# Expert blocks of two halves in turns, and each weight fetch issued between a block's products and its bias add

## The chip, the cores and the metric

One core of one Trainium2 chip runs the whole program. The metric is the device time of one execution in microseconds (us). The engines named below are PE (TensorE, matrix products), DVE (VectorE), ACT (ScalarE), POOL (GpSimd, which here mainly issues transfers) and SP (SyncE, transfers only). Each engine works through its own queue in order. A difference of about 0.3% is what a measurement of this kernel can tell from none.

## The reference, cut to what matters

Eight items of 256 channels by 32x32 positions go through a multi-head attention layer with a residual, then through a single-head attention layer, then through a mixture of experts. The last part is the one that the change touches:

```python
logits = tokens @ router_w.T                 # 8 experts
probs = softmax(logits); rw, re = top_k(probs, 2); rw = rw / rw.sum(-1)
combine = zeros((N, E)).at[arange(N)[:, None], re].set(rw)
out = tokens
for e in range(8):
    h = gelu(tokens @ w1[e] + b1[e], approximate=False)   # 256 -> 256
    y = h @ w2[e] + b2[e]                                 # 256 -> 256
    out = out + combine[:, e:e + 1] * y
```

A token is one position of one item, 1024 tokens an item. Each token needs only the two experts that its router chose. The setup makes `b1` and `b2` all zeros.

## The kernel before, in words

Items 0 to 7 are worked on one after the other: `layer0` (the multi-head attention), `attend` (the single-head one), `normed` and the router. For items 0 to 6 `dispatch` (L847) scatters each token's normalised row twice, once for each chosen expert, into a DRAM buffer `rows` that has one region for each expert. The eighth item isn't dispatched: its experts are computed densely at the end (`dense`), every expert for every token.

In the middle of item 7's `layer0` the function `plan` (L924) cuts the filled part of each region into blocks of 256 rows, on DVE, from the counts. Their number is only known on the chip, so the program has a fixed number of positions, `group.nb` = 63, and `plan` fills two tables: `row_at`, the first row of the block at each position, and `w_at`, the rows of the packed weights `wpack` to fetch for it. Blocks stand in the order of their experts: all blocks of expert 0, then all of expert 1, and so on.

`experts` (L1018) then runs the positions b = 0 to 62. Per position:

- `fetch` (L1036): SP reads the block's start and loads its 256 rows in four transfers into `xr` (four buffers).
- `weights` (L1025): POOL issues one indirect transfer of 128 rows of 5128 bytes (both matrices and both biases of one expert, 656,384 bytes) into buffer b mod 4 of `wbs_x` (`wb` three times, `wb_x`). If the block four positions earlier belonged to the same expert, the buffer already holds the right weights; `plan` then sets the indices out of bounds (L979, L982), and the transfer is issued but moves no rows. Below this is called a skipped fetch, the other a real one.
- `turned` (L1047): DVE turns `xr` into `xb` (two buffers).
- `hidden` (L1056): PE makes 8 products into `ph` (L1061), ACT applies the Gelu (L1071).
- `collect` (L1080): PE makes 8 products into `pe` (L1087, two buffers in PSUM), DVE adds the bias `b2` out of the same `wb` buffer and writes `yb` (L1097, two buffers), POOL issues the store of `yb` into the DRAM buffer `y` (L1102). Then one step of `places` may run.

The loop at the end of `experts` sets the order by hand, and `tc.issue_after` pins some instructions:

```python
for b in range(group.nb + 4):
    if b - 3 in rows: hiddens[b - 3], last = hidden(b - 3, rows.pop(b - 3))
    if b < group.nb:  rows[b] = fetch(b)
    if b - 1 in rows: weights(b - 1)
    if b - 2 in rows: rows[b - 2], squares = turned(b - 2, rows.pop(b - 2))
    if b - 4 in hiddens: collect(b - 4, hiddens.pop(b - 4), last, squares)
```

So PE does the hidden products of position k+1, then the second products of k, then the hidden ones of k+2, and so on. On POOL the fetch for position k+4 stands behind the store of position k. The framework adds the waits from the order in which the code reads and writes each buffer: a fetch into a buffer waits for its earlier readers, and a reader waits for the last fetch that the code wrote above it.

`places` (L991) works out, on DVE, in which row of `y` each token's two results lie. It is a generator that gives way after each of its 14 pieces (7 items, 2 choices), 5 small instructions each; one piece runs in the iterations from position 4 on. Later, in item 7's last part, `Results` gathers these rows from `y` by POOL's indirect transfers (L1181) and adds them to the tokens.

Of the kernel before, what the change touches and what calls it, by code (L numbers as in the profile page):

```python
# [10 lines left out]
F32 = mybir.dt.float32  # L11
I32 = mybir.dt.int32
AF = mybir.ActivationFunctionType
ALU = mybir.AluOpType
# [5 lines left out]
def kernel(  # L20
# [23 lines left out]
    nc = tc.nc  # L44
    P = 128
    B, C, S = x.shape
    E, D, FF = w1.shape
# [4 lines left out]
    NT = S // P  # L52
# [5 lines left out]
    BR = R * P  # L58
    WROW = NCC * FF + NFC * D + NFC + D
    NWB = 3  # L60
    NXB = NWB + 1
    SQ = 32
    NQ = P // SQ
    DQ = D // NQ
    RUN = BR // SQ

    dram = ctx.enter_context(tc.tile_pool(name="dram", bufs=1, space=bass.MemoryType.DRAM))
    const = ctx.enter_context(tc.tile_pool(name="const", bufs=1))
# [4 lines left out]
    small = ctx.enter_context(tc.tile_pool(name="small", bufs=6))  # L73
    rowp = ctx.enter_context(tc.tile_pool(name="rowp", bufs=4))
    keep = ctx.enter_context(tc.tile_pool(name="keep", bufs=8))
# [64 lines left out]
    for e in range(E):  # L140
# [6 lines left out]
    NBMAX = max(2 * len(g) * S // BR + E - 1 for g in GROUPS)  # L147
    b_iota = const.tile([P, NBMAX], F32, name="b_iota")
    nc.gpsimd.iota(
        b_iota, [[1, NBMAX]], base=0, channel_multiplier=0, allow_small_or_imprecise_dtypes=True  # L150
    )
    p_iota = const.tile([P, 1], F32, name="p_iota")
    nc.gpsimd.iota(
# [10 lines left out]
        base=0,  # L164
        channel_multiplier=-1,
# [758 lines left out]
    def plan(group):  # L924


        n, nb, cap = group.n, group.nb, group.cap
        counts = group.counts
        steps = cap // BR

        def tmp(tag, shape, dtype=F32):
            return small.tile([P, *shape], dtype, tag=tag, name=f"{tag}_{n}", bufs=1)


        below = tmp("p_below", [E, steps])
        edge = tmp("p_edge", [steps])
        nc.vector.tensor_scalar_mul(edge, b_iota[:, :steps], float(BR))
        nc.vector.tensor_tensor(
            below,
            counts.unsqueeze(2).to_broadcast([P, E, steps]),  # L940
            edge.unsqueeze(1).to_broadcast([P, E, steps]),
            ALU.is_gt,
        )
        blocks = tmp("p_blocks", [E])
        nc.vector.tensor_reduce(blocks, below, AX.X, ALU.add)
        ends = tmp("p_ends", [E])
        nc.vector.tensor_tensor_scan(ends, ones[:, :E], blocks, 0.0, ALU.mult, ALU.add)
        first = keep.tile([P, E], F32, tag="first", name=f"first_{n}", bufs=2)
        nc.vector.tensor_sub(first, ends, blocks)

        mine = tmp("p_mine", [nb, E])
        of = b_iota[:, :nb].unsqueeze(2).to_broadcast([P, nb, E])
        nc.vector.tensor_tensor(
            mine, of, ends.unsqueeze(1).to_broadcast([P, nb, E]), ALU.is_ge
        )
        e_of = tmp("p_e", [nb])
        nc.vector.tensor_reduce(e_of, mine, AX.X, ALU.add)
        nc.vector.tensor_scalar_min(e_of, e_of, float(E - 1))
        nc.vector.tensor_tensor(
            mine,  # L960
            e_of.unsqueeze(2).to_broadcast([P, nb, E]),
            e_iota.unsqueeze(1).to_broadcast([P, nb, E]),
            ALU.is_equal,
        )

        base = tmp("p_base", [E])
        nc.vector.tensor_scalar_mul(base, first, -float(BR))
        work = tmp("p_work", [nb, E])
        lo, hi = tmp("p_lo", [nb]), tmp("p_hi", [nb])
        nc.vector.tensor_mul(work, mine, base.unsqueeze(1).to_broadcast([P, nb, E]))  # L970
        nc.vector.tensor_reduce(lo, work, AX.X, ALU.add)
        nc.vector.scalar_tensor_tensor(lo, b_iota[:, :nb], float(BR), lo, ALU.mult, ALU.add)
        nc.vector.tensor_scalar_min(lo, lo, float(cap - BR))
        nc.vector.scalar_tensor_tensor(lo, e_of, float(cap), lo, ALU.mult, ALU.add)
        row_at = keep.tile([P, NBMAX], I32, tag="row_at", name=f"row_at_{n}", bufs=2)
        nc.vector.tensor_copy(row_at[:, :nb], lo)
        nc.vector.tensor_scalar(hi, e_of, float(P), p_iota, ALU.mult, ALU.add)
        same = tmp("p_same", [nb])
        nc.vector.tensor_tensor(  # L979
            same[:, NXB:], e_of[:, NXB:], e_of[:, : nb - NXB], ALU.is_equal  # L980
        )
        nc.vector.scalar_tensor_tensor(  # L982
            hi[:, NXB:], same[:, NXB:], float(E * P), hi[:, NXB:], ALU.mult, ALU.add
        )
        w_at = keep.tile([P, NBMAX], I32, tag="w_at", name=f"w_at_{n}", bufs=2)
        nc.vector.tensor_copy(w_at[:, :nb], hi)

        group.first = first
        group.where = row_at, w_at

    def places(group):  # L991

        first = group.first
        for b in group.items:
            gate, kept = group.kept[b]
            ats = []
            for k, (row, exp) in enumerate(kept):
                hot = small.tile([P, NT, E], F32, tag="d_sel", name=f"p_hot_{b}_{k}", bufs=1)
                nc.vector.tensor_tensor(
                    hot,  # L1000
                    exp.unsqueeze(2).to_broadcast([P, NT, E]),
                    e_iota.unsqueeze(1).to_broadcast([P, NT, E]),
                    ALU.is_equal,
                )
                nc.vector.tensor_mul(
                    hot, hot, first.unsqueeze(1).to_broadcast([P, NT, E])
                )
                to = small.tile([P, NT], F32, tag="d_to", name=f"p_to_{b}_{k}", bufs=2)
                nc.vector.tensor_reduce(to, hot, AX.X, ALU.add)
                nc.vector.scalar_tensor_tensor(to, to, float(BR), row, ALU.mult, ALU.add)  # L1010
                at = keep.tile([P, NT], I32, tag=f"yat{k}", name=f"yat{k}_{b}")
                nc.vector.tensor_copy(at, to)
                ats.append(at)
                if k > 0:
                    group.kept[b] = gate, ats
                yield

    def experts(group, behind):  # L1018
        n = group.n
# [5 lines left out]
        def weights(b):  # L1025
            wb = wbs_x[b % NXB]
            nc.gpsimd.indirect_dma_start(
                out=wb[:, :],
                out_offset=None,
                in_=wpack[:, :],  # L1030
                in_offset=bass.IndirectOffsetOnAxis(ap=w_at[:, b : b + 1], axis=0),
                bounds_check=E * P - 1,
                oob_is_err=False,
            )
# [45 lines left out]
        def collect(b, hT, last, squares):  # L1080
            wb = wbs_x[b % NXB]
            py = acc(f"pe_{n}_{b}")
            at = NCC * FF
            with tc.issue_after(last.ins):
                for r in range(R):
                    for fc in range(NFC):
                        nc.tensor.matmul(  # L1087
                            py[:, ts(r, D)],
                            hT[:, fc, ts(r, P)],
                            wb[:, at + fc * D : at + (fc + 1) * D],  # L1090
                            start=(fc == 0),
                            stop=(fc == NFC - 1),
                        )
            at += NFC * D + NFC
            yb = two.tile([P, R, D], F32, tag="yb", name=f"yb_{n}_{b}")
            with tc.issue_after(squares.ins):
                added = nc.vector.tensor_add(  # L1097
                    yb,
                    py.rearrange("p (r d) -> p r d", d=D),
                    wb[:, at : at + D].unsqueeze(1).to_broadcast([P, R, D]),  # L1100
                )
            nc.gpsimd.dma_start(group.y[ts(b, BR), :].rearrange("(r p) d -> p r d", r=R), yb)  # L1102
            if b >= NXB:
                with tc.issue_after(added.ins):
                    next(placed, None)


        rows, hiddens = {}, {}
        placed = places(group)
        assert group.nb - NXB >= 2 * len(group.items)  # L1110
        last = squares = None
        for b in range(group.nb + 4):
            if b - 3 in rows:
                hiddens[b - 3], last = hidden(b - 3, rows.pop(b - 3))
            if b < group.nb:
                rows[b] = fetch(b)
            if b - 1 in rows:
                weights(b - 1)
            if b - 2 in rows:
                rows[b - 2], squares = turned(b - 2, rows.pop(b - 2))  # L1120
            if b - 4 in hiddens:
                collect(b - 4, hiddens.pop(b - 4), last, squares)
# [247 lines left out]
    for b in range(B):  # L1370
# [6 lines left out]
        if b + 1 < B:  # L1377
            begun = Begin(b + 1, next_x)
            t2 = attend(b, t1, begun.at)
            n2, _, l = normed(b, t2, begun.at)  # L1380
# [61 lines left out]
```

## Time and profile before

| what | us |
|---|---|
| time of the kernel, median of 3 runs (2348.14 to 2354.57) | 2354.15 |
| the profiled execution's own time | 2357.7 |
| its span, first to last instruction | 2355.1 |
| the expert stage: from the second products of position 0 to those of position 62 | 1885.8 to 2129.8 |
| PE busy in that stage of 244.0 | 222.4 |
| DVE / ACT / POOL busy in that stage | 97.4 / 54.8 / 108.5 |

The granted TensorE clock was 0.990 over the span. A row of the profile names the line, the engine, the operation and the tiles (written<-read); "idle before" is the time the engine waited ahead of it, and the name behind the arrow is what ended that wait. The chain of waits is followed back from the last instruction and printed in order of time: start, length, what. A transfer that POOL issues shows on POOL only as the time of its issue; its data and its completion come later.

### The profile page before, as it was taken

What the parts mean: (1) busy time and instruction counts of PE and PEld (TensorE: products, weight loads), DVE (VectorE), ACT (ScalarE), POOL (GpSimd) and SP (SyncE); (2) the same over time, 40 slices, a digit from 0 to 9 for tenths busy, and PEclk for the clock granted to TensorE, in tenths of its full rate; (3) what the DMA queues carried; (4) which work ended last, traced back from release to release, by engine and by line L of the source; (5) the groups of instructions that cost most, each with busy time, mean ns of one, the idle gap of its engine ahead of it and who ended that gap; (6) DMA issues with size and microseconds to landing.
All of it is one profiled execution on the core that took longest, in us unless ns stands there. A gap on an engine that the chain in (4) does not pass through costs nothing.

```text
span 2355.1 us, 37660 instructions
## 1 busy us (share of the span) xinstructions
PE 2282.4 (97%) x13123; PEld 1230.8 (52%) x13123; DVE 1512.9 (64%) x3660; ACT 1093.5 (46%) x1955; POOL 409.9 (17%) x390
## 2 busy tenths in 40 slices
PE   9999999999999999999999999999999998989698
PEld 3345534653456345633563356335643477776465
DVE  5775578557855785578557865786578653335755
ACT  3663366346634663466346635563555521223311
POOL 0000012000200020002000300030003044445563
PEclk9999999999999999999999999999999999999799
DMA  8995201020102010201020102000201268765564
GB/s 294 385 386 143 64 17 40 12 52 13 44 8 56 10 46 5 59 8 48 1 51 15 53 1 45 19 35 3 45 19 59 55 196 221 210 198 160 158 206 116
DMA packets 278756, 209.25 MB, mean 89 GB/s; under 512 B 187784, under 2 KB 230440, under 8 KB 276776
## 3 DMA queue, kind: packets, MB, share of 16 engines
q1 hardware_dynamic: 252472, 139.14, 21.0%
q0 software_dynamic: 25008, 67.20, 8.8%
q8 instruction: 104, 1.70, 0.3%
q10 hardware_dynamic: 1088, 0.52, 0.1%
q14 instruction: 84, 0.69, 0.1%
HBM read 108.88 MB, written 110.90 MB: 93 GB/s over the span
## 4 chain that ended last, share of the span: by engine, by line
PE 87%; DVE 4%; DMA 3%; issue 3%; ACT 1%; POOL 1%; SPq 0%; another core or an unknown queue 0%; DVEq 0%; POOLq 0%; ACTq 0%
PE po L539 19%; PE psc L462 18%; PE ps L670 9%; PE py L711 8%; PE pqk L344 7%; PE pr L636 5%; PE pv L381 4%; PE ph L1061 4%; PE pe L1087 3%; PE pdh L1308 2%; PE pdy L1332 2%; PE px L655 2%; DMA wb<-wpack,w_at 2%; PE pqk L322 2%; DVE n L236 1%
## 5 line engine op out<-in xcount | busy, mean ns | idle before, releaser
L503 ACT ACTIVATE ex<-psc,nmax 128x1024 f32<-128x1024 f32 x512 | 570.5, 1115 | 307.2 <-DVE scrap L486 220.9
L462 PE MATMUL psc<-qk,qk 64*64 64x512 f32 x4096 | 574.1, 593 | 3.4 <-ACT ex L503 3.3
L539 PE MATMUL po<-ex,vs 64*64 64x512 f32 x4096 | 569.6, 593 | 7.5 <-SPq L549 6.6
L486 DVE TENSOR_SCALAR_CACHE_REDUCE scrap<-psc,nmax 128x512 f32<-128x512 f32 x512 | 384.5, 751 | 163.9 <-PE psc L462 137.3
L477 DVE TENSOR_REDUCE nmax<-psc 128x1 f32<-128x512 f32 x512 | 350.7, 685 | 9.5 <-PE psc L462 9.5
L462 PEld LDWEIGHTS psc<-qk,qk 64*64 64x64 f32 x4096 | 178.8, 132 | 281.1 <-ACT ex L503 131.8
L539 PEld LDWEIGHTS po<-ex,vs 64*64 64x64 f32 x4096 | 173.4, 132 | 283.9 <-issue 84.2
L711 PE MATMUL py<-n,aT 128*128 128x256 f32 x1024 | 234.3, 383 | 4.5 <-DMA aT<-sq 4.5
L670 PE MATMUL ps<-nT,xa 128*128 128x512 f32 x512 | 228.5, 592 | 0.0
L711 PEld LDWEIGHTS py<-n,aT 128*128 128x128 f32 x1024 | 196.4, 193 | 54.9 <-issue 27.6
L915 POOL DMA_INDIRECT rows<-n,d_at x112 | 109.2, 975 | 661.4 <-DVE nmax L477 661.1
L695 ACT COPY aT<-sq 32x256 f32<-32x256 f32 x384 | 154.4, 402 | 79.8 <-DVE sq L688 52.3
L842 POOL TENSOR_TENSOR t<-t,n 128x2048 f32<-128x2048 f32 x8 | 36.3, 4535 | 879.2 <-DVE n L236 879.2
L344 PE MATMUL pqk<-xT,wqkv 128*128 128x512 f32 x384 | 171.2, 599 | 0.0
L670 PEld LDWEIGHTS ps<-nT,xa 128*128 128x128 f32 x512 | 96.6, 190 | 102.4 <-issue 95.1
L678 DVE TENSOR_REDUCE nmax<-ps 128x1 f32<-128x1024 f32 x64 | 77.9, 1217 | 88.3 <-PE ps L670 82.6
L309 ACT ACTIVATE qk<-pqk,b_qks 128x512 f32<-128x512 f32 x124 | 85.6, 690 | 95.8 <-PE pqk L344 77.0
L381 PE MATMUL pv<-wqkv,xT 128*128 128x512 f32 x256 | 121.5, 603 | 2.6 <-ACT wqkv L110 1.7
L1181 POOL DMA_INDIRECT yk<-y,yat x112 | 110.7, 988 | 74.6 <-issue 32.3
L344 PEld LDWEIGHTS pqk<-xT,wqkv 128*128 128x128 f32 x384 | 71.0, 190 | 99.9 <-issue 76.8
L1061 PE MATMUL ph<-xb,wb 128*128 128x256 f32 x384 | 95.3, 392 | 18.5 <-DMA wb<-wpack,w_at 15.6
L636 PE MATMUL pr<-wo,res 128*128 128x256 f32 x512 | 111.9, 379 | 0.0
(188 smaller groups left out, 2320.7 us busy)
## 6 DMA issues: line engine op xcount, KB each, us to landing
rows<-wb SPq DMA_DIRECT2D x7, 8192.0 KB
xr<-rows SPq DMA_DIRECT2D x252, 64.0 KB
y<-yb POOLq DMA_DIRECT2D x63, 256.0 KB
aT<-sq SPq DMA_DIRECT2D x384, 32.0 KB
xs<-in_x_dram SPq DMA_DIRECT2D x64, 128.0 KB
out_dram<-oT SPq DMA_DIRECT2D x60, 128.0 KB
xT<-in_x_dram SPq DMA_DIRECT2D x7, 1024.0 KB
sums<-t SPq DMA_DIRECT2D x7, 1024.0 KB
```

The costliest lines, as they stand in the source:

```text
L344: mm = nc.tensor.matmul(pq[:, ts(n, 512)], wqkv[:, cc, t, ts(g, P)], xT[:, cc, ts(n, 512)], start=(cc == 0), stop=(cc == NCC - 1),)
L381: nc.tensor.matmul(pv, self.xT[:, cc, ts(i, P)], wqkv[:, cc, 2, :], start=(cc == 0), stop=(cc == NCC - 1),)
L462: mm = nc.tensor.matmul(pss[at, h][ts(c, DK), ts(n, 512)], k[r, j * P + c * DK : j * P + (c + 1) * DK], q[r, ts(n, 512)], start=True, stop ...
L477: firsts[at, h] = nc.vector.tensor_reduce(nmax, pss[at, h][:, ts(0, 512)], AX.X, ALU.max, negate=True)
L486: seconds[h] = nc.vector.tensor_scalar(scrap, pss[at, h][:, ts(1, 512)], -1.0, nmaxes[at, h], ALU.mult, ALU.min, accum_out=nmax,)
L503: nc.scalar.activation(ex, pss.pop((at, h)), AF.Exp, bias=nmaxes.pop((at, h)), scale=1.0, accum_out=sums[at][:, h : h + 1],)
L539: mm = nc.tensor.matmul(po[n][ts(h, DK), :], vss[at][keys, h, :], exps[at, h][keys, ts(n, 512)], start=(j == 0 and turn == 0), stop=(j == ...
L636: nc.tensor.matmul(pr[:, :C], res[:, g, ts(i, P)], wo[:, g, :], start=(g == 0), stop=(g == NPAIR - 1))
L670: nc.tensor.matmul(psc[:, ts(n, 512)], xa[:, ec, ts(i, P)], nT[:, ec, ts(n, 512)], start=(ec == 0), stop=(ec == NCC - 1),)
L695: move(to[ts(k, SQ), a], since[ts(a, SQ), k])
L711: nc.tensor.matmul(py[:, :D], aT[m], n1[:, m, :], start=(m == 0), stop=(m == NT - 1))
L1061: last = nc.tensor.matmul(ph[:, ts(fc, BR)], wb[:, dc * FF + fc * P : dc * FF + (fc + 1) * P], xb[:, dc, :], start=(dc == 0), stop=(dc == ...
```

## The change

`plan` orders the blocks anew: position 0 takes the first block of experts 0 to 3, position 1 the first of experts 4 to 7, position 2 the second of experts 0 to 3, and so on, until one half has no blocks left; the rest of the other half follows. `left` is the number of blocks of experts 0 to 3. `places` counts with the new positions, in two pieces for each item and choice (28 in all). In `experts` the fetch for position b+4 moves into `collect(b)`, between the products and the bias add; the loop itself only issues the first four.

```diff
+    WHOLE = 1.5 * 2**23
+    half_iota, odd_iota = ...      # two more constant tiles, POOL iota, at the start
 def plan(group):
         nc.vector.tensor_sub(first, ends, blocks)
+        left = ends[:, E // 2 - 1 : E // 2]
+        right = tmp("p_right", [1])
+        nc.vector.tensor_sub(right, ends[:, E - 1 : E], left)
+        turns = keep.tile([P, 1], F32, tag="turns", name=f"turns_{n}", bufs=2)
+        nc.vector.tensor_tensor(turns, left, right, ALU.min)
+        nc.vector.tensor_tensor(rest, right, left, ALU.is_gt)
+        nc.vector.tensor_mul(rest, rest, left)
+        nc.vector.tensor_sub(rest, rest, turns)
+        nc.vector.tensor_add(twice, turns, turns)
+        nc.vector.scalar_tensor_tensor(block, odd, left, half, ALU.mult, ALU.add)
+        nc.vector.tensor_scalar_add(after, b_iota[:, :nb], rest)
+        nc.vector.tensor_scalar(taking, b_iota[:, :nb], twice, None, ALU.is_lt)
+        nc.vector.tensor_sub(block, block, after)
+        nc.vector.tensor_mul(block, block, taking)
+        nc.vector.tensor_add(block, block, after)
-        of = b_iota[:, :nb].unsqueeze(2).to_broadcast([P, nb, E])
+        of = block.unsqueeze(2).to_broadcast([P, nb, E])
...
-        nc.vector.scalar_tensor_tensor(lo, b_iota[:, :nb], float(BR), lo, ALU.mult, ALU.add)
+        nc.vector.scalar_tensor_tensor(lo, block, float(BR), lo, ALU.mult, ALU.add)
...
+        nc.vector.tensor_scalar(first[:, E // 2 :], first[:, E // 2 :], left, None, ALU.subtract)
-        group.first = first
+        group.first = first, turns
 def places(group):
                 nc.vector.scalar_tensor_tensor(to, to, float(BR), row, ALU.mult, ALU.add)
+                yield
+                pos = small.tile([P, 2, NT], F32, tag="d_pos", name=f"p_pos_{b}_{k}", bufs=2)
+                nc.vector.tensor_scalar(pos[:, 0], to, 0.5 - BR / 2, 1.0 / BR, ALU.add, ALU.mult)
+                nc.vector.tensor_scalar_add(pos[:, 0], pos[:, 0], WHOLE)
+                nc.vector.tensor_scalar(pos[:, 1], exp, E / 2 - 0.5, None, ALU.is_gt)
+                nc.vector.scalar_tensor_tensor(pos[:, 0], pos[:, 0], -WHOLE, pos[:, 1], ALU.add, ALU.add)
+                nc.vector.tensor_scalar(pos[:, 0], pos[:, 0], turns, float(BR), ALU.min, ALU.mult)
+                nc.vector.tensor_add(to, to, pos[:, 0])
 def collect(b, hT, last, squares):
...                                            # the 8 products into py
+            if b + NXB < group.nb:
+                weights(b + NXB)
             at += NFC * D + NFC
             yb = two.tile([P, R, D], F32, tag="yb", name=f"yb_{n}_{b}")
             with tc.issue_after(squares.ins):
                 added = nc.vector.tensor_add(yb, py..., wb[:, at : at + D]...)
             nc.gpsimd.dma_start(group.y[ts(b, BR), :]..., yb)
...                                            # the loop
-            if b - 1 in rows:
+            if b - 1 in rows and b - 1 < NXB:
                 weights(b - 1)
```

More of the change, by code (lines that the diff above doesn't have):

```diff
@@ L150 @@
         b_iota, [[1, NBMAX]], base=0, channel_multiplier=0, allow_small_or_imprecise_dtypes=True
+    )
+    HALVES = (NBMAX + 1) // 2
+    half_iota = const.tile([P, HALVES, 2], F32, name="half_iota")
+    nc.gpsimd.iota(
+        half_iota,
+        [[1, HALVES], [0, 2]],
+        base=0,
+        channel_multiplier=0,
+        allow_small_or_imprecise_dtypes=True,
+    )
+    odd_iota = const.tile([P, HALVES, 2], F32, name="odd_iota")
+    nc.gpsimd.iota(
+        odd_iota,
+        [[0, HALVES], [1, 2]],
+        base=0,
+        channel_multiplier=0,
+        allow_small_or_imprecise_dtypes=True,
     )
@@ L949, in plan @@
         nc.vector.tensor_sub(first, ends, blocks)
+        left = ends[:, E // 2 - 1 : E // 2]
[3 more added lines that the diff above has]
+        nc.vector.tensor_tensor(turns, left, right, ALU.min)
+        rest = tmp("p_rest", [1])
+        nc.vector.tensor_tensor(rest, right, left, ALU.is_gt)
+        nc.vector.tensor_mul(rest, rest, left)
+        nc.vector.tensor_sub(rest, rest, turns)
+        twice = tmp("p_twice", [1])
+        nc.vector.tensor_add(twice, turns, turns)
+        block = tmp("p_block", [nb])
+        after = tmp("p_after", [nb])
+        taking = tmp("p_taking", [nb])
+        half = half_iota.rearrange("p h t -> p (h t)")[:, :nb]
+        odd = odd_iota.rearrange("p h t -> p (h t)")[:, :nb]
+        nc.vector.scalar_tensor_tensor(block, odd, left, half, ALU.mult, ALU.add)
[4 more added lines that the diff above has]
+        nc.vector.tensor_add(block, block, after)
         mine = tmp("p_mine", [nb, E])
-        of = b_iota[:, :nb].unsqueeze(2).to_broadcast([P, nb, E])
+        of = block.unsqueeze(2).to_broadcast([P, nb, E])
         nc.vector.tensor_tensor(
@@ L986, in plan @@
         nc.vector.tensor_copy(w_at[:, :nb], hi)
-        group.first = first
+        nc.vector.tensor_scalar(
+            first[:, E // 2 :], first[:, E // 2 :], left, None, ALU.subtract
+        )
+        group.first = first, turns
         group.where = row_at, w_at
     def places(group):
-        first = group.first
+        first, turns = group.first
         for b in group.items:
@@ L1010, in places @@
                 nc.vector.scalar_tensor_tensor(to, to, float(BR), row, ALU.mult, ALU.add)
+                yield
+                pos = small.tile([P, 2, NT], F32, tag="d_pos", name=f"p_pos_{b}_{k}", bufs=2)
+                nc.vector.tensor_scalar(
+                    pos[:, 0], to, 0.5 - BR / 2, 1.0 / BR, ALU.add, ALU.mult
+                )
+                nc.vector.tensor_scalar_add(pos[:, 0], pos[:, 0], WHOLE)
+                nc.vector.tensor_scalar(pos[:, 1], exp, E / 2 - 0.5, None, ALU.is_gt)
+                nc.vector.scalar_tensor_tensor(
+                    pos[:, 0], pos[:, 0], -WHOLE, pos[:, 1], ALU.add, ALU.add
+                )
+                nc.vector.tensor_scalar(
+                    pos[:, 0], pos[:, 0], turns, float(BR), ALU.min, ALU.mult
+                )
+                nc.vector.tensor_add(to, to, pos[:, 0])
                 at = keep.tile([P, NT], I32, tag=f"yat{k}", name=f"yat{k}_{b}")
@@ L1109, in experts @@
         placed = places(group)
-        assert group.nb - NXB >= 2 * len(group.items)
+        assert group.nb - NXB >= 4 * len(group.items)
         last = squares = None
```

## The prediction

> **What bounds the kernel now.** I read the engines' line first, then three windows, then the chain of waits, then single rows. PE is busy nearly always:
>
> ```profile
> PE 2282.4 (97%) x13123; PEld 1230.8 (52%) x13123; DVE 1512.9 (64%) x3660; ACT 1093.5 (46%) x1955; POOL 409.9 (17%) x390
> ```
>
> The windows (us, then busy time and instructions of PE, PEld, DVE, ACT, POOL, then clock, DMA share, GB/s) split the span before, in and after the expert stage:
>
> ```profile
> 0.00:1885.80 1885.80, 1864.39 (x11450) 916.18 (x11451) 1279.62 (x3171) 983.85 (x1724) 185.46 (x155) 1.00 0.22 65
> 1885.80:2129.80 244.00, 222.44 (x995) 188.86 (x994) 97.37 (x202) 54.83 (x127) 108.52 (x121) 0.99 0.73 207
> 2129.80:2355.10 225.30, 195.53 (x682) 125.71 (x680) 135.92 (x288) 54.86 (x104) 115.96 (x115) 0.93 0.57 159
> ```
>
> The change works in the middle one. There the chain is PE, block after block, broken where weights are fetched:
>
> ```profile
> 1906.89 8.99 DMA wb<-wpack,w_at
> ...
> 1916.02 1.97 PE ph L1061 x8
> 1917.98 1.73 PE pe L1087 x8
> 1919.71 1.73 PE ph L1061 x8
> 1921.43 1.73 PE pe L1087 x8
> ...
> 1935.61 5.51 DMA wb<-wpack,w_at
> ```
>
> A block costs PE 2 x 1.73 = 3.455 us; 63 blocks are 1.73 + 62 x 3.455 = 215.9. The stage takes 244.0, so **28.1 us are stalls** around the fetches. That is all a better fetch order could win. Evaluating the reference's router on its inputs gives items 0 to 6 7, 8, 8, 7, 8, 8, 8, 7 blocks for experts 0 to 7: 61, in 63 positions. Every change of expert refills four buffers, 8 x 4 = 32 real fetches; the trace's DMA records show just 32 bursts of 128 packets of 5128 bytes.
>
> **The new wait.** Look at what the bias add waits for today and at POOL's queue around it:
>
> ```profile
> 1921.80 1.05 POOL L1027 DMA_INDIRECT wb<-wpack,w_at  x1 [0.30 <-PE ph L1061]
> ...
> 1923.20 0.69 DVE L1097 TENSOR_TENSOR yb<-pe,wb 128x512 f32<-128x512 f32 x1 [1.00 <-PE pe L1087]
> ...
> 1924.19 0.75 POOL L1102 DMA_DIRECT2D y<-yb  x1 [1.34 <-DVE p_hot L999]
> ...
> 1925.24 1.04 POOL L1027 DMA_INDIRECT wb<-wpack,w_at  x1 [0.30 <-PE ph L1061]
> ```
>
> The add starts when its products end; the store follows it by 0.99 us, the next fetch follows the store by 1.06 (1920.73 to 1921.80 the step before). In the new code the fetch for position k+4 is written above the add of position k, and both use the same `wb` buffer, out of which the add reads `b2`. So the add now reads what that fetch writes: it must wait until the fetch has *landed*. The instruction streams of the new kernel as built confirm it: the add of block 12 waits for the fetch of position 16. Skipped fetches count too, since they also complete by semaphore.
>
> Behind the waiting add on DVE stand the pieces of `places` and the turn of block k+3; behind the waiting store on POOL stands the next fetch. From position 10 on POOL's stream is fetch k+4, store k, fetch k+5, store k+1. That closes a ring: fetch issued, landed (L), add, store, next fetch. Its turn is L + 0.05 + 0.99 + 1.06 = **L + 2.10**, against PE's 3.455. (For the blocks before, fetch k+5 stands ahead of store k, and the turn k+4 ahead of add k: PE stays the bound.)
>
> **L from the trace.** From POOL's issue to the last semaphore landing, the 29 skipped fetches of this stage from 1896 on took 2.14 to 4.38 us, median 3.2; the two near 1921.80 and 1925.24, 3.06 and 2.54. The dear ones sit behind real fetches in the same queue. The new pace loads the queues less, so I take **3.0**, ends 2.14 and 3.5. First real fetches of a burst took 5.0 to 7.3, most of them 5.0 to 6.0 (the chain's row above: 5.51). In the new order real ones come two positions apart or more, with a pair next to each other now and then: I take **5.45**, ends 5.0 and 6.5.
>
> A plain store lands no faster, as the last one before the gathers shows (issued 2130.82, the gather released 2133.61):
>
> ```profile
> 2130.82 0.71 POOL L1102 DMA_DIRECT2D y<-yb  x1 [0.97 <-DVE yb L1097]
> 2133.61 1.00 POOL L1181 DMA_INDIRECT yk<-y,yat  x1 [2.08 <-DMA y<-yb]
> ```
>
> The Trainium skill, "DMA: Bandwidth & Descriptors", section "Anatomy of one DMA — SWDGE (gpsimd) path", gives about 2.0 us fixed plus bytes / 436e3 for such a transfer. By it L would be 2.0 skipped and 3.5 real, and the sum below some 60 us smaller. No row here is that quick, and the rows decide.
>
> **Real fetches after.** Half A (experts 0 to 3) has 30 blocks, half B 31. Each half owns two of the four buffers, so a change of expert refills two: positions 14, 16, 30, 32, 46, 48 for A, 17, 19, 33, 35, 49, 51 for B, and 60, 62 where B's rest takes over A's buffers. 14, after the first four: 18 instead of 32.
>
> **The sum, on the profiled execution (2357.7).**
> - Position 0's second products end at 1887.54; position 9's at 1887.54 + 9 x 3.455 = 1918.6; fetch 13 is issued at 1918.9.
> - To fetch 62 are 49 turns of 5.1, 249.9, of which 13 with a real fetch cost 2.45 more, 31.9: 2200.7.
> - It lands after 5.45; add 0.74, turn of block 61 0.81, its hidden products 1.97, four more product groups 6.92: 2216.6, against 2129.8. That is **+86.8**: the old stalls are contained in the comparison, nothing is subtracted twice.
> - `plan`: 13 more small DVE instructions in a chain. Here PE is idle 4.28 us waiting for plan's end (SP's queue, which releases it, holds the read of `row_at`):
>
> ```profile
> 1806.61 0.21 DVE L982 SCALAR_TENSOR_TENSOR p_hi<-p_same,p_hi 128x59 f32<-128x59 f32 x1
> 1806.74 0.21 DVE L972 SCALAR_TENSOR_TENSOR p_lo<-b_iota,p_lo 128x63 f32<-128x63 f32 x1
> ...
> 1808.71 1.98 PE L539 MATMUL po<-ex,vs 64*64 64x512 f32 x8 [4.28 <-SPq L549]
> ```
>
>   Neighbours there start 0.13 to 0.25 apart; at 0.2 that is **+2.6** (1.7 to 3.3), on the path.
> - `places`: 14 more steps of 6 further instructions each, 0.2 apart. On DVE a step of 7 takes 1.45 beside add 0.69 and turn 0.71: 2.85 of a turn of 5.1. Nothing, with POOL's ring as cover. Without it the loop over PE decides (products k, fetch, landing, add, step, turn, hidden and second products of k+3 and k+2, two blocks): 0.1 + 3.0 + 0.1 + 0.69 + 1.45 + 0.71 + 0.1 + 1.97 + 1.73 = 9.85, or 4.9 a block, just under the ring.
> - The two more iotas on POOL run at the start beside loads: nothing; at most their issue, under 1 us. The last part of the kernel keeps its streams: nothing, 1 us either way.
>
> In all +89.4: 2447.1 on the profile's own scale. The median of the runs lies 3.55 below the profiled time, so the forecast is **2444**.
>
> Ends: with 2.14 and 5.0 the ring (4.24) falls under the loop with a step (4.5), which blocks 10 to 31 have: 22 x 4.5 + 27 x 4.24 + 13 x 2.86 = 250.7, the last landing 5.0, in all +55.3 and 1.7 for plan: 2411. With 3.5 and 6.5: 49 x 5.6 + 13 x 3.0 = 313.4, the last landing 6.5, in all +119.4 and 3.3: 2477.
>
> **Rivals.**
> - *The fetches are fewer and nothing else matters* (faster). 14 spread fetches hide, the 28.1 of stalls go, plan costs 2.6: 2329. For it: fetches spaced two blocks apart have 6.9 us of PE work each. Against: it needs the add not to wait, that is L below 3.455 - 2.10 = 1.35, and no fetch is under 2.14. 4%.
> - *Only the real fetches cost* (slower, less): skipped ones land within the slack. 14 x (7.55 - 3.455) = 57.3, less 28.1, plus 2.6: 2386. Same point of decision, L = 1.35. 7%.
> - *Transfers collide*: each fetch stands behind a store and beside the loads of `xr`, and L is as in the old bursts, 4.1 skipped, 7.2 real: 49 x 6.2 + 13 x 3.1 = 344.1, end 7.2, +153 with plan: 2507. Against: these were fetched back to back. 8%.
> - *The order isn't what the counts say* and 32 fetches stay real: 14 x 2.45 = 34 more: 2478. 1%.
>
> **How the numbers follow.** Forecast 80%, 2444, with 2411 to 2477 from the ends. The range 2405 to 2482 leaves out the first, second and third rivals, 19%. Faster by over 0.3% only in the first rival: 0.04; within 0.3%: 0.01; slower: 0.95.
>
> **What would show it.** After: the add's idle time ends on a DMA into `wb`, not on PE `pe`; PE's share in the stage falls to about 215 of 331 us; POOL's fetches come 5.1 us apart from position 14 on, but 3.5 before; 18 bursts of weights. Wrong if the add still waits for PE, or the fetches come 3.5 or over 6 us apart.

## The result, and the profile after

The changed kernel takes 2462.28 us (median of 4 runs, 2459.27 to 2463.96) against 2352.62 (4 runs, 2348.14 to 2354.57) for the kernel before on the same chip: 1.0468 times as long, 95% interval 1.0448 to 1.0487. The forecast was 2444 with a range of 2405 to 2482. The profiled execution took 2462.89, its span is 2461.1 and its granted clock 0.979 (0.990 before).

First the engines' line of the page, then the three windows of the new trace (columns as in the prediction):

```profile
PE 2311.3 (94%) x13123; PEld 1246.1 (51%) x13123; DVE 1529.7 (62%) x3757; ACT 1093.5 (44%) x1955; POOL 411.6 (17%) x392
```

```profile
0.00:1888.00 1888.00, 1863.86 (x11450) 916.81 (x11451) 1280.97 (x3184) 983.83 (x1724) 186.20 (x157) 1.00 0.22 65
1888.00:2236.00 348.00, 252.39 (x990) 203.45 (x989) 113.07 (x286) 54.83 (x127) 107.90 (x120) 0.91 0.42 118
2236.00:2461.00 225.00, 195.07 (x687) 125.81 (x685) 135.69 (x288) 54.85 (x104) 117.50 (x115) 0.94 0.57 159
```

The first stretch is 2.2 us longer than before (1888 against 1885.8; `plan` runs in it) and the last one as long (225.0 against 225.3). Only the expert stage has grown much, from 244 to 348 us, with the same products on PE (990 records against 995; some can be missing) and, in the third last column, a granted clock of 0.91 in place of 0.99. PE's busy time there is higher by 30 us only because the same products ran slower; a share of busy time would hide that.

What the bias add (now L1157) waits for, from the costliest groups by shape:

```profile
L1157 DVE TENSOR_TENSOR yb<-pe,wb 128x512 f32<-128x512 f32 x48 | 33.2, 691 | 172.7 <-DMA wb<-wpack,w_at 151.4 <-PE pe L1145 15.9 <-issue 5.3
L1157 DVE TENSOR_TENSOR yb<-pe,wb_x 128x512 f32<-128x512 f32 x15 | 10.3, 689 | 52.7 <-DMA wb_x<-wpack,w_at 48.8 <-PE pe L1145 3.9
```

Before, DVE's waiting ahead of this add ended on PE's products (us in total, times, longest):

```profile
DVE yb L1097 <- PE pe L1087: 141.2, 62, 6.7
```

Now 200.2 us of it (151.4 + 48.8) ends on a transfer into the same weight buffer. The chain of waits goes the way the prediction drew it, here around the fetches of positions 12 and 14:

```profile
1918.11 2.16 DMA wb<-wpack,w_at
...
1920.40 0.69 DVE yb L1157
...
1921.94 0.72 DVE xb L1108
...
1922.71 3.23 PE ph L1119 x8
1925.94 2.19 PE pe L1145 x8
...
1928.89 4.62 DMA wb<-wpack,w_at
...
1933.64 0.69 DVE yb L1157
```

Read it downwards: a fetch lands, the add runs, the turn of a later block (L1108) that stood behind it on DVE runs, PE gets its hidden products, then the second ones, and only these let the next fetch of the chain go (it overwrites the weights that they read). PE, which was the chain itself before, is now one link of a loop. The two product groups take 3.23 and 2.19 us here, against 1.97 and 1.73 in the rows of before.

Later, with no `places` step behind the add, the ring on POOL that the prediction named stands bare in the timeline (start, length, engine and line, idle time before it):

```profile
2180.18 1.06 POOL L1085 DMA_INDIRECT wb_x<-wpack,w_at  x1 [0.30 <-issue]
...
2183.40 0.69 DVE L1157 TENSOR_TENSOR yb<-pe,wb_x 128x512 f32<-128x512 f32 x1 [3.95 <-DMA wb_x<-wpack,w_at]
...
2184.39 0.74 POOL L1162 DMA_DIRECT2D y<-yb  x1 [3.15 <-DVE yb L1157]
...
2185.44 1.07 POOL L1085 DMA_INDIRECT wb<-wpack,w_at  x1 [0.31 <-issue]
```

Fetch issued (position 55, a skipped one), 3.22 until the add starts, 0.99 until the store's issue, 1.05 until the next fetch: 5.26 us, for a fetch that moves no rows. The trace has 18 bursts of 128 packets of 5128 bytes where there were 32, and the queue that carries them moved 58.01 MB instead of 67.20, 14 x 0.656 less. The change does what it says; the smaller traffic bought nothing here.

One more thing follows from the add reading behind the fetch: the `b2` that it adds is the one that lies in the buffer after the fetch for position b+4, and behind a real fetch that is another expert's. As `b2` is all zeros in this setup, no result shows it; with other biases the changed kernel would add wrong ones.

### The profile page after: what moved, and what is told of

It is laid out like the page before. It is cut to its first block, busy times and chain, and to the rows that moved or that the text cites. A ratio compares the mean times of both kernels' runs of the same rounds, so it can differ in the third digit from the quotient of the medians.

```text
span 2461.1 us, 37736 instructions
## 1 busy us (share of the span) xinstructions
PE 2311.3 (94%) x13123; PEld 1246.1 (51%) x13123; DVE 1529.7 (62%) x3757; ACT 1093.5 (44%) x1955; POOL 411.6 (17%) x392
## 3 DMA queue, kind: packets, MB, share of 16 engines
q0 software_dynamic: 25008, 58.01, 7.2%
## 4 chain that ended last, share of the span: by engine, by line
PE 77%; issue 9%; DVE 5%; POOL 4%; DMA 3%; ACT 1%; another core or an unknown queue 0%; SPq 0%; DVEq 0%; POOLq 0%; ACTq 0%
PE po L557 18%; PE psc L480 17%; PE ps L688 8%; PE py L729 8%; PE pqk L362 7%; PE pr L654 5%; PE pv L399 4%; PE px L673 2%; PE ph L1119 2%; POOL yk L1241 2%; PE pqk L340 2%; PE pe L1145 2%; DMA wb<-wpack,w_at 1%; POOL wb L1085 1%; DVE n L254 1%
## 5 line engine op out<-in xcount | busy, mean ns | idle before, releaser
L1119 PE MATMUL ph<-xb,wb 128*128 128x256 f32 x384 | 108.8, 432 | 73.4 <-DVE xb L1108 72.0
L1157 DVE TENSOR_TENSOR yb<-pe,wb 128x512 f32<-128x512 f32 x48 | 33.2, 691 | 172.7 <-DMA wb<-wpack,w_at 151.4
L1129 ACT ACTIVATE hb<-ph,wb 128x256 f32<-128x256 f32 x96 | 40.4, 471 | 218.1 <-issue 218.1
L1119 PEld LDWEIGHTS ph<-xb,wb 128*128 128x128 f32 x384 | 78.9, 213 | 99.8 <-DVE xb L1108 85.4
```

Source lines behind the costliest of these rows:

```text
L1119: last = nc.tensor.matmul(ph[:, ts(fc, BR)], wb[:, dc * FF + fc * P : dc * FF + (fc + 1) * P], xb[:, dc, :], start=(dc == 0), stop=(dc == ...
```

## The experiments

Each is compared with the kernel before on the same chip. In the first four that kernel took 2358.57 us, 6 us more than on the chip of the result, whose scale the expected times have: there, the ratios and the stages are the better guide. "Stage" is the stretch from the first second products (`pe`) to the first product of the last part (`pt_n`); it is 244.0 in before and 348.9 in after.

### The two halves of the change apart

**The fetch moved alone.** The loop and `collect` of the new kernel in the old one; the blocks stay in the order of their experts.

```diff
 # before, collect(b), above the bias add
+            if b + NXB < group.nb:
+                weights(b + NXB)
 # the loop
-            if b - 1 in rows:
+            if b - 1 in rows and b - 1 < NXB:
```

> The kernel before, in its order of experts, with only the fetch moved above the add. New wait theory: the ring of fetch, landing, add and store as in the changed kernel, with 28 real fetches in place of 14, each about 2.3 us dearer in the ring; plan's 2.2 are not there and places has 14 short pieces: 2462 + 32 - 2 = 2490, at least 2470. Theory that the turns or the longer places cost the time: near the kernel before, 2352 to 2370.

Measured: 2496.92 us, 1.0593 of before (1.0569 to 1.0617); stage 380.5. The window of the stage:

```profile
1885.00:2265.00 380.00, 265.91 (x992) 210.96 (x991) 97.31 (x204) 54.82 (x127) 107.92 (x120) 0.89 0.45 133
```

The move alone is worse than the whole change, by 31.6 us of stage: 14 more real fetches at the prediction's 2.45 each would be 34.

**The turns alone.** The new order of blocks and the new `places`, with the fetch back in the loop, ahead of the turn.

```diff
 # after
-            if b + NXB < group.nb:
-                weights(b + NXB)
-            if b - 1 in rows and b - 1 < NXB:
+            if b - 1 in rows:
```

> The new order of blocks and the 28 pieces of places, but the fetch where it was before (in the loop, behind the store). New wait theory: no wait on a landing in the add; real fetches come 2.1 us after the products, land 7.1 to 7.6 after them against 6.9 of cover, so each of the 14 stalls by 0.2 to 0.7 us: about 2335 to 2340, between the first kernel of this call and the kernel before. Theory that the turns cost: about 2440.

Measured: 2345.94 us, 0.9958 (0.9944 to 0.9973); stage 225.4. The turns are a small gain (0.4%), the move a large loss.

### What of the move costs

**The fetch under the add**, two lines lower than in the change: above the store still, but no longer above the reader of `b2`.

```diff
 # after, collect(b)
-            if b + NXB < group.nb:         # ahead of the add
-                weights(b + NXB)
             added = nc.vector.tensor_add(yb, ...)
+            if b + NXB < group.nb:
+                weights(b + NXB)
             nc.gpsimd.dma_start(group.y[...], yb)
```

> The changed kernel with the fetch for position b+4 written below the bias add of block b and above its store; all else as changed. The new wait theory: the add reads what no later fetch writes, so it waits for PE again, and the fetch waits for the add. It is issued about 1.0 us after the block's products end (before: 2.1), and the hidden products that need it start 6.9 us after them; a real fetch of 5.0 to 5.5 lands in time. The 28 us of stalls go, plan's 2.2 stay: about 2331, and no stall of PE above 1 us on a weight fetch. The theory that the turns or the transfers themselves are slow (more switches, fetches beside stores): the loss stays, about 2440 or more.

Measured: 2345.27 us, 0.995 (0.9932 to 0.9968); stage 224.4. One statement's place is worth some 5% (1.0468 against 0.995), or 124.5 us of stage. The expected 2331 would have been 0.991: the loss goes, but the gain is smaller than expected. The fetch is now the add's successor in the buffer instead of its source. The stage is still 8.5 us over the 215.9 of PE alone: PE stands 12 times for 0.23 to 1.32 us ahead of its hidden products, 10 of them until a real weight fetch lands. The chain shows what makes fetches late:

```profile
1937.40 7.15 DMA wb<-wpack,w_at
...
1994.45 9.03 DMA y<-yb x2
...
2052.65 9.21 DMA y<-yb x2
```

A store issued behind a fetch that moves 656 KB lands late, and `yb` has two buffers: the add two blocks on waits for it (44.5 us of the add's waiting in this stage), and the next fetch here waits for that add.

**The wait taken away, the place kept.** The add reads a constant tile of zeros instead of `b2`; fetches and stores are issued in the order of the change.

```diff
 # after
+    no_bias = const.tile([P, D], F32, name="no_bias")
+    nc.gpsimd.memset(no_bias, 0.0)
-            wb[:, at : at + D].unsqueeze(1).to_broadcast([P, R, D])
+            no_bias.unsqueeze(1).to_broadcast([P, R, D])
```

> The changed kernel with the fetch where the change put it, but the add reads its bias from a constant tile of zeros and not out of the weights' buffer (it leaves out b2, which the inputs make zero). The queue order and the fetches are those of the changed kernel; only the reason to wait is gone. New wait theory: the add waits for PE alone, fetches are issued about 0.3 us after the products: 2328 to 2332. Theory that the earlier fetch collides with the store in POOL's queue or among the transfers: the loss stays above 2400.

Measured: 2339.53 us, 0.9916 (0.9896 to 0.9935). Its stage:

```profile
1888.00:2104.00 216.00, 214.45 (x993) 188.05 (x992) 110.83 (x287) 54.83 (x127) 108.19 (x121) 1.00 0.71 191
```

216.2 us against the ideal 215.9 of PE alone. Without the wait for the landing all of the stage's growth is gone, so it belongs to that wait. The old stalls are gone as well; they were PE's waits for the weights of a new expert, and fetches that are fewer, apart and early cover them. The run also ends the rival in which transfers collide: the same transfers in the same order on the same queue cost nothing once the add does not wait for them. The clock is back at 1.00.

**The ring opened.** The store of `yb` is issued by SP, so POOL's next fetch no longer stands behind it.

```diff
-            nc.gpsimd.dma_start(group.y[...], yb)
+            nc.sync.dma_start(group.y[...], yb)
```

> The changed kernel with the store of y issued by SP and not by POOL. The add still waits for the fetch's landing, but the next fetch no longer stands behind the store. Ring theory (POOL's ring of fetch, landing, add, store sets the pace where no piece of places runs, the loop over PE where one does): only the loop is left, about 4.1 us a block without a piece, 4.9 with one, real fetches weigh half as each of two interleaved loops meets every second one: 2462 less some 45 to 58, about 2405 to 2417. Theory that the loop over PE, slowed by the lower clock, sets the pace everywhere: little change, 2445 to 2465.

Measured: 2433.96 us, 1.0341 (1.032 to 1.0361): 28 us less than the change, where 45 to 58 were expected; a miss in size. The stage is 315.3. What POOL's fetch waits for here, and what the add does (us in total, times, longest):

```profile
POOL wb L1085 <- PE pe L1145: 126.0, 27, 9.3
DVE yb L1157 <- DMA wb<-wpack,w_at: 109.8, 33, 10.2
```

The add still waits for landings, and the fetch now waits for PE where it waited for the store. So the ring goes and the loop over PE, which the prediction put at 4.9 a block with a `places` step, takes over almost at once. In the late steps without one, many fetches alternate between some 4.9 and 3.45 us apart, 4.2 in the mean of such pairs; over all steps, real fetches included, the mean is 125.6 / 23 = 5.5 in the positions 13 to 35 and 5.1 in 36 to 61.

### Why it cost 17 us more than forecast

From span to span the sum was 16.6 us short. The steps behind skipped fetches were longer than in it: by 10.6 us in all in the positions 13 to 35, which carry `places` steps, and by 9.2 in the positions 36 to 61 (the table further down has the sum by term). In the early ones POOL's fetch waits for PE at 10 of 23 positions, and PE's groups are slow. From the new kernel's timeline, PE's hidden products after different waits:

```profile
1969.40 3.78 PE L1119 MATMUL ph<-xb,wb 128*128 128x256 f32 x8 [4.68 <-DVE xb L1108]
...
1981.55 3.56 PE L1119 MATMUL ph<-xb,wb 128*128 128x256 f32 x8 [2.47 <-DVE xb L1108]
...
1992.80 1.99 PE L1119 MATMUL ph<-xb,wb 128*128 128x256 f32 x8 [2.52 <-DVE xb L1108]
```

Of the 52 whole groups of 8 that the timeline shows from 1918 to 2236, the 30 with under 1.8 us of idle time ahead took 1.89 to 1.99; all 10 with over 3.1 took 2.84 to 3.78; of 12 between 1.89 and 2.75, 5 took 2.81 to 3.67 and 7 took 1.99. The Trainium skill, "TensorE: Matmul & The Clock Gate", section "HAM oscillation — how this bites in real kernels", has the rule that PE must have no idle gaps above about 3.4 us, or its clock halves. The 8 gaps over 3.4 us here agree; the 7 slow groups behind 1.89 to 3.40 us of idle time do not fit the limit. The trace's clock record shows more. The granted clock is either full or half, for stretches of 3.41 us or multiples of it. Around the first slow group, two such stretches read (length, PE's busy time, ..., the clock third last):

```profile
1919.90:1923.31 3.41, 1.52 (x8) 1.01 (x7) 2.15 (x6) 0.12 (x1) 1.76 (x3) 1.00 0.24 79
1923.31:1926.72 3.41, 3.41 (x10) 2.70 (x9) 2.42 (x9) 0.69 (x2) 0.79 (x2) 0.50 0.80 226
```

PE was busy for 45% of one (1.52 of 3.41 us), and the clock was halved in the next. All 14 halvings between 1920 and 2220 follow a stretch with PE busy for 45% or less, and of the stretches that full clock followed only one was below that (42%). So in this trace the clock goes with PE's busy share in fixed stretches of 3.41 us, and the length of a single gap counts only through that share.

Is the slow clock the cause of the dear steps, or a by-product? Three kernels keep PE busy with products whose result nothing reads, from position 8 on:

```diff
 # after, hidden(b)
+            if b >= 8:
+                for _ in range(6):         # 2 and 3 in the other two
+                    nc.tensor.matmul(ph[:, 512:768], scrap[:, :P], scrap[:, :BR], start=True, stop=True)
```

> The changed kernel with six extra products of 128x256 (1.3 us of PE) on constant data ahead of the hidden products of each block from 8 on; they go into a part of the block's PSUM tile that is not read, and wait for no transfer. Clock theory (the 18 us that the prediction missed come from the granted clock of 0.90 in the waiting stretch, which makes a group of 8 products last up to 3.8 us instead of 1.73 and lengthens the loop over PE): the clock rises to 0.97 or more, steps of blocks 18 to 35 fall from 5.8 to about 5.0, the time falls by 8 to 16, to 2446 to 2454, although PE has 73 us more to do. Rival (landings were simply later than taken, the clock beside the path): the same time, 2462, or up to 10 more.

Measured: 2477.96 us, 1.053 (1.0509 to 1.0551). Inconclusive: a product of 256 columns in this type runs as two records of 0.216 (a group of 8 in the rows above is four products), so 6 of them took 2.59 us and not 1.3. PE needed 3.455 + 2.59 = 6.05 a block, and the steps from fetch 13 to 62 became 6.25 in the mean. The clock rose to 0.993 over the span, but PE had become the bound.

> The new kernel with 2 extra products (0.86 us at full clock) in front of each block's hidden products from position 8 on, into columns of the product tile that nothing reads; PE per block 4.3, under the ring's 5.1. Theory (the granted clock falls to 0.84 to 0.94 because PE stands idle in the waits, and this makes the steps with pieces 5.8 instead of 5.0): the clock in the stage rises to 0.95 or more, groups of 8 hidden products take about 1.75 again, and some 5 to 16 us go: 2446 to 2457. Rival (the clock is a by-product and PE is never late): 2462, and as the extra work is on the loop over PE, up to 0.86 for each of 23 positions with pieces, 2480.

> The same with 3 extra products (1.3 us), PE per block 4.75. Theory: the clock is higher still than with 2, but the loop over PE grows by up to 0.65 to 1.3 a position where the extra products do not fit into PE's idle time: 2446 to 2466. Rival: 2470 to 2490.

Measured: 2460.47 us with two (1.0442, 1.0413 to 1.0471), 2459.96 with three (1.0446, 1.0416 to 1.0477). Neither can be told from the change itself (1.0448 to 1.0487): by ratio they lie 5 to 6 us below it, within the intervals. Inside, more can be seen. The stretches are those from fetch 13 to 28, to 38 and to 62 in after (the clock is the third last column); first of after, then of the kernel with two:

```profile
1921.60:2012.20 90.60, 64.64 (x240) 51.55 (x240) 36.41 (x116) 12.59 (x30) 27.79 (x31) 0.87 0.42 116
2012.20:2077.10 64.90, 44.97 (x163) 36.15 (x164) 22.75 (x66) 8.40 (x20) 18.06 (x20) 0.84 0.43 122
2077.10:2220.10 143.00, 97.26 (x386) 76.71 (x385) 31.42 (x48) 20.15 (x48) 43.36 (x49) 0.94 0.38 110
```

```profile
1921.60:2012.20 90.60, 77.01 (x327) 64.54 (x326) 36.34 (x115) 13.44 (x32) 28.61 (x32) 0.94 0.43 120
2012.20:2077.10 64.90, 50.37 (x200) 41.45 (x199) 23.71 (x70) 8.39 (x20) 18.34 (x21) 0.89 0.44 122
2077.10:2220.10 143.00, 116.88 (x494) 94.81 (x493) 31.46 (x49) 20.15 (x48) 44.86 (x50) 0.96 0.38 112
```

The clock went from 0.87 and 0.84 to 0.94 and 0.89, and the 15 skipped steps of the positions 13 to 35 from 5.80 to 5.40 on average (5.40 with three as well): 23 steps took 139.8 instead of 144.2 us. So the clock is part of the cause by these traces, 4.4 us of it with a third to a half of the dip gone; each is a single execution, and the change's own runs spread over 4.7 us. Of that the extra products gave 2.6 back in the positions 8 to 13, where PE is the bound (33.6 us instead of 31.0 from fetch 4 to 13). The expected 5 to 16 us did not show.

**The pieces of places later.**

```diff
 # after, collect(b)
-            if b >= NXB:
+            if b >= 30:
                 with tc.issue_after(added.ins):
                     next(placed, None)
```

> The new kernel with one number changed: the pieces of places run at positions 30 to 57 instead of 4 to 31. Theory (in the positions with pieces the ring of the fetch's landing and the loop over PE, with its slowed product groups, take turns in setting the pace; elsewhere the ring alone, L + 2.10): the granted clock falls and POOL's fetches wait for PE in the positions from about 40 on in place of 13 to 35; a step without a real fetch takes about 5.2 in the early part instead of 5.8, and about 5.8 in the late one instead of 5.25. More positions of the waiting part then carry pieces (28 instead of about 23), so the stage is equal or up to 5 us longer: 2460 to 2468. Rival (the early positions are slow for another reason, such as the change of experts' rows being closer together there or the chip's state after plan): early steps stay at 5.8, late ones rise too, and the time is 2470 to 2480. A third, that pieces cost nothing anywhere, as the prediction had it: no step changes.

Measured: 2463.78 us, 1.0467 (1.0431 to 1.0504). The stage is 345.4 against 348.9, not longer. The clocks by stretch, as above:

```profile
1921.60:2012.20 90.60, 60.41 (x247) 47.92 (x248) 19.63 (x30) 12.59 (x30) 28.29 (x32) 0.96 0.40 118
2012.20:2077.10 64.90, 43.13 (x161) 34.03 (x160) 17.52 (x42) 8.40 (x20) 18.38 (x21) 0.89 0.43 125
2077.10:2220.10 143.00, 100.11 (x386) 79.70 (x385) 57.70 (x180) 20.16 (x48) 43.32 (x48) 0.90 0.40 110
```

The dip moved with the pieces (0.96 early and 0.90 late, 0.87 and 0.94 before), and so did POOL's waits for PE, which now lie at 2070 to 2200. The price did not follow. Early skipped steps take 5.44 without pieces, where 5.2 was expected, and late ones 5.53 with them, as in the change (5.54), where 5.8 was expected. With the real fetches, the 23 early steps took 142.6 us instead of 144.2 and the 26 late ones 154.1 instead of 154.3. The reason shows in the landings: with pieces most skipped fetches land in 2.2 to 2.7 us and the loop over PE decides; without, most in 3.0 to 3.4 and the ring decides. The two take turns at nearly the same price. My theory was right on where the wait sits, wrong on the pieces being what makes it dear; the rival (early positions slow for another reason) falls too, as the early steps fell from 5.80 and the late ones did not rise. The third, that the pieces cost nothing, is nearest to what was measured.

### Early fetches without the wait

ACT copies `b2` into a tile of its own (two buffers) behind the Gelus, and the add reads the copy. That keeps the early fetch and the right bias. Once with the old order of blocks (the kernel before with the fetch moved as in the change), once with the turns; the diff leaves out that `b2s` starts as an empty dict:

```diff
 # hidden(b), behind the Gelus
+            b2s[b] = two.tile([P, D], F32, tag="b2", name=f"b2_{n}_{b}", bufs=2)
+            at += NFC
+            nc.scalar.copy(b2s[b], wb[:, at : at + D])
 # collect(b), the add's second operand
-            wb[:, at : at + D].unsqueeze(1).to_broadcast([P, R, D])
+            b2s.pop(b).unsqueeze(1).to_broadcast([P, R, D])
```

> The kernel before, in its order of experts, with the fetch moved above the add, but the add reads the bias from a small copy that ACT makes earlier from the weights' buffer. So the fetch is issued some 1.8 us earlier than before and nobody waits for its landing. If the earlier issue is worth as much as the lead that it gives, each of the 7 changes of expert stalls 1.8 us less, 12 to 13 in all: a ratio of about 0.995. If the four fetches in a row are held by the transfers (4 us each against 3.455 of PE), less: 0.998. The turns' own worth is what lies between this kernel and the next.

> The changed kernel, complete, with the bias read from a small copy made by ACT (both things that the change sets out to do, without the new wait). As the kernel with the constant bias: stage of 217 us, ratio to the kernel before about 0.991 to 0.992; faster than the fetch below the add (0.995) by some 5 us.

Measured: old order 2342.23 us, 0.9951 (0.9934 to 0.9968), stage 230.0; turns 2335.25 us, 0.9921 (0.9905 to 0.9936), stage 218.9, the best complete version here. The stage of the latter:

```profile
1889.50:2108.40 218.90, 215.25 (x993) 187.96 (x992) 113.00 (x287) 79.42 (x188) 108.35 (x120) 1.00 0.69 188
```

The early fetch wins 14 us of the stage with 32 real fetches (244.0 to 230.0), and 6.5 more than the turns alone when combined with them (225.4 to 218.9). The idea of the change was sound on both counts; only the operand that the add reads undid it, in time and in what it adds.

## Why the prediction was right, point by point

- **The mechanism** held: the add waits for the landing (200.2 us of its idle time), skipped fetches count, the trace shows 18 bursts, the fetches come 3.45 apart up to position 13 and slow down there. Fetch 13 was issued at 1921.57; the sum gave 1918.9 plus plan's 2.6.
- **The sum** was 16.6 us short, +89.4 against +106.0 from span to span. By term:

| term | predicted | measured |
|---|---|---|
| `plan`, on the path (first `pe` 1888.01 against 1885.81) | +2.6 | +2.2 |
| position 0 to fetch 13 | 31.4 | 31.8, 0.5 more |
| 13 turns behind a real fetch | 7.55 each | 7.32 each, 3.0 less in all |
| 15 turns behind a skipped one, positions 13 to 35 | 5.1 each | 5.80 each, 10.6 more |
| 21 turns behind a skipped one, positions 36 to 61 | 5.1 each | 5.54 each, 9.2 more |
| fetch 62 to the stage's end | 15.9 | 16.8 |
| last part | 0 | -1.1 |

- **What it left out** is the clock. It took PE at full speed, "about 215 of 331 us"; PE was busy for 252.4 of 348. And its mark against itself, fetches "over 6 us apart", is touched: from fetch 13 to 62 they came 6.1 apart in the mean, 5.65 behind skipped ones, where its sum has 5.75 and 5.1.
- **The step that was mis-sized** is "49 turns of 5.1": L of 3.0 for a skipped fetch, and the loop over PE at 4.9 "just under the ring". The bare ring of the late steps is 5.15 to 5.36 for most, as L is 3.0 to 3.35 there; that is 0.15 or so a turn. Four turns between 2066 and 2089 alternate between 7.0 to 7.9 and 4.3 to 4.4, and three skipped fetches took 4.0 to 4.3. In the positions 13 to 35 L was smaller than taken (2.1 to 2.8, median 2.5), yet the loop was the longer one: its 9.85 for two blocks had product groups at 1.97 and 1.73, and the groups behind long waits took up to 3.78. The open-ring kernel shows that the loop by itself holds the stage at 315; the kernels with extra products show some 4.4 us of the excess to come from the clock. The rest of the 19.8 is divided only by argument. Nor do the steps divide cleanly into skipped and real ones: four of the 15, next to real fetches (positions 13, 15, 31 and 34), took 6.5 to 7.3 and hold 7.5 of the 10.6.
- **Luck** has a part in the range. Its upper end, 2477, came from an L of 3.5. L was below that for all but four of the skipped fetches from 13 on, and the excess came by the loop over PE, to which the sum gave no spread for slow products.
- **The real fetches** were slightly over-priced: the 14 landed in 4.45 to 6.42, median 5.06, against 5.45 taken. (The row of 5.51 that it points to is the second fetch of its burst and not the first.)
- **`plan`** was right: PE's idle time there is 6.93 instead of 4.28, on the same releaser:

```profile
1811.17 1.98 PE L557 MATMUL po<-ex,vs 64*64 64x512 f32 x8 [6.93 <-SPq L567]
```

- **`places` at nothing** held in effect: shifting all pieces by 26 positions changed the time by nothing that can be told.
- **The rivals.** Faster (the add needn't wait) and slower by real fetches alone both need skipped fetches to land in under 1.35; none landed under 2.09. Collisions are refuted by the kernel that keeps the transfers and drops the wait, and 32 real fetches by the 18 bursts.
- **What stays open.** The last part took 224.3 us in after, 225.5 in before, 225.0 and 225.4 in two variants (old order with copied bias, late pieces), but 227.0 to 232.8 in six others, with nothing changed in it (the kernels with extra products order the end of the stage differently and are left aside). In the part's middle the granted clock falls to 0.7 to 0.9 in before, in after and in three of the six alike; whether the difference comes from there is not shown. It eats up to 7 us of what the stage gained (the variant without `b2` won 27.8 in the stage and 18.0 in its span), and nothing here was run to settle it. Nor is it settled why a skipped fetch lands in 2.1 us in one place and in 3.3 in another.

## What to carry to other kernels

A prefetch into a buffer may be issued early only if every reader of the old contents is written above it; otherwise the reader becomes a reader of the prefetch: it waits for its landing and gets its contents. Ask this of the small riders in a packed buffer (here 256 biases of a 656 KB fetch), which are read last; a copy into a tile of their own costs ACT 0.4 us a block and frees the buffer early. And a transfer that is skipped by its indices is not free for whoever waits for it: its time from issue to landing is what counts, and around a loop that time is paid at every turn.

## What the runs showed of the hardware

- An indirect fetch whose indices are all out of bounds took 2.09 to 4.25 us (median 2.6) from issue to completion, against 4.45 to 6.42 (median 5.06) for one that moved 656 KB: moving nothing saves about half.
- PE's granted clock was halved for 3.41 us or multiples of it, each time after a stretch of 3.41 us in which PE was busy for 45% or less (14 of 14 halvings from 1920 to 2220); a gap of 1.89 us was enough in one case. A group of 8 records then took up to 3.78 us instead of 1.89 to 1.99.
- Filling part of the idle time with spare products raised the clock from 0.87 to 0.94 and from 0.84 to 0.89 in the two slow stretches; the time did not fall by more than the intervals.
- A store that is issued behind a 656 KB fetch on the same queue held its buffer for 4.2 to 5.6 us where the chain of the kernel with the fetch under the add shows single ones; the last store in the trace of before, alone in its queue, was done in 2.8.
- On DVE the instruction of `places` that takes a per-partition scalar from a tile (L1065, 128x8) took 0.49 us in 11 of its 14 executions in after, and 0.23 in the other 3 and in all 14 of the kernel with the turns alone; its neighbours of the same shape take 0.16 to 0.17. What made it longer is open.
